# A four-layer block on one core: where the next batch's inputs, the shared expert and the output are put

## The chip, the core and the metric

The kernel runs on one core of one Trainium2 chip. The core has a matrix engine (TensorE, in the profile PE), a vector engine (VectorE, DVE), an engine for activation functions (ScalarE, ACT), a general one (GpSimd, POOL) and a queue engine (SyncE, SP), each with its own instruction queue worked off in order; sixteen DMA engines move data. PE reads from the on-chip memory SBUF and writes to PSUM, which has eight banks of 128 partitions by 512 float32. The metric is the device time of one execution in microseconds, the median of three runs.

## The reference

Four residual steps over x of shape (4, 512, 512) in float32: an attention, a gated feed-forward net with ternary weights, a state-space scan, and a second attention followed by a mixture of experts.

```python
def reference(...):
    x = L0_attn_x                                   # (4, 512, 512) float32
    x = x + _L0_attn_ref(_layernorm(x), W_qkv, W_o)           # 16 heads of 32, rotary, causal
    x = x + _L0_ffn_ref(_layernorm(x), w1, w3, w2)            # ternary weights, hidden 1365
    x = x + _L1_attn_ref(_layernorm(x), W_xproj, W_dt, b_dt, A_log, D_param)
    x = x + _L1_ffn_ref(_layernorm(x), ...)

# _L0_ffn_ref
g = silu(x @ w1q.T) * (x @ w3q.T);  return g @ w2q.T

# _L1_attn_ref: a scan over the tokens, 16 states per channel
delta = softplus((xz[..., :128] @ W_dt.T) + b_dt)
h = exp(delta * A) * h + delta * B_t * x_t;  y_t = sum(h * C_t);  return y + x * D_param

# _L1_ffn_ref: attention with a latent, then a mixture of experts
h = x + attention(rmsnorm(x, ln1_w), ...)
out = h + moe(rmsnorm(h, ln2_w), ...)
# moe: a shared expert for every token, and the 2 best of 7 experts, weighted
expert_ffn(x, wg, wu, wd) = (silu(x @ wg) * (x @ wu) / 8) @ wd        # inner size 256
return shared + combined
```

## The kernel before

B = 4 batches of T = 512 tokens with C = 512 channels; P = 128, and NT = NK = 4 tiles of tokens or channels. The residual x of batch b lies in SBUF as `xs[b]` all the time. The kernel is written in a framework that places the waits itself. Where a block stands under `manual_schedule(engines={PE})`, PE's instructions keep the order of the program; the other engines get an order from the framework's planner, which starts what is ready by its own estimate, earlier program text first. That order is then fixed. Every helper whose work is spread over a stage is a Python generator: each `next` emits the instructions up to its next `yield`, at that place of PE's order. PSUM is cut into two pairs of banks (`pair`, also `half_pair`, the first bank of a pair) and four single ones (`bank`); a new tile of a kind waits until one of its places is free.

**First attention** (0 to 430 us): not touched.

**Feed-forward** (430 to 751 us, lines 594 to 715). For each batch b and each of NF = 11 slices f of the hidden size, `gated` multiplies into the two banks of a pair `pg` (gate, then up; L651, 16 records, high and low parts), ACT applies Silu (L656), DVE multiplies (L657), and the product is cut into a high and a low part (L662, L663); `down` of the slice before adds into four banks `ys` (L669). `part(n)` is called three times a slice: n = 3f between gate and up, 3f + 1 after up, 3f + 2 after down. It advances `between`, which is `prepare(b - 1, ...)` (lines 495 to 588): the preparation of the scan for the batch before. `prepare` normalises (`make`), transposes (L131), projects (`pd`, `pb`, `pz`: L520, L529, L551), and computes softplus with Exp (L555), three DVE operations per channel tile on a tile `u` (L559 to L561), Ln (L563), and `finish` (L568 to L571: delta, its store, the product `ux`); `turn_out` transposes ux (L576), copies it to the one buffer `st` and stores it (L579). Those of Exp, Ln and Silu that follow one another on ACT load another table each time (1.28 us). `coming` is `inputs(b + 1)`, the norm and the transposes (`tpf`, L633) of the next batch's inputs; it is advanced once at the end of each slice from f = 4 on, right after part(3f + 2). In batch 3 there is no next batch, and `part` leaves out n = 2 only.

**Scan** (751 to about 1120 us, lines 812 to 971): 128 steps (batch, state, half). `prepare` of batch 3 goes on inside it: two of its pieces and then five stand ahead of the first step, one more after every second step.

**Second attention** (to about 1624 us). `soften`, `turn` and `weigh` run over 128 pairs of heads. `leave(b, oT)` follows for the batch before: four output projections (L1031), h = h + y (L1034), a store of h to the DRAM tensor `acc` (L1036), the square sum (L1038), the norm with ln2 (L1045), transposes, the store to `hrows` and the router. At the very end stand two pieces of `leave(3)`, then `shared(0)`, then the rest of `leave(3)`.

**Shared expert** `shared(b)` (lines 979 to 1009): transposes h by token tiles into hT, for each of two halves i of the inner size gate and up in the two banks of one pair (L990, eight records each), Silu (L995), product (L997); then four down projections (L1004) and the addition to xs[b] (L1008). `shared(1)` and `shared(2)` run beside the routing work.

**Routed experts** (about 1682 to 1905 us): 38 tiles of 128 places. For each, GpSimd gathers rows of `hrows` (L1386), PE runs the expert, and GpSimd adds the weighted rows to `acc` with an accumulating scatter (L1427); scatters follow one another. Here PE isn't ordered by hand. **The end:** `shared(3)`, and for each of 16 token tiles a load of `acc` on SP (L1449), an addition to xs (L1450), and a store to `out` on ACT's queue (L1451), all ordered by the planner.

## Time and profile before

| what | us |
|---|---|
| median of three runs (1941.34 to 1942.90) | 1942.84 |
| the profiled execution | 1946.77 |
| its span | 1945.0 |
| PE busy | 1764.7 |
| DVE busy | 1145.5 |
| ACT busy | 948.2 |
| GpSimd busy | 580.9 |
| PE waits in 425 to 745 us for DVE's sil | 8.0 |
| PE waits for ACT's hid / hTe in the shared experts | 4.4 / 4.5 |

In a line of the timeline stand the start, the duration, the engine, the line of the program, the operation, output and inputs, how many are merged, and in brackets how long the engine stood idle before it and who released it. Float32 matmuls over 512 columns appear as two records of some 0.43 us each; in the feed-forward stage one record is issued every 0.233 us. In a row of a stretch stand its length, busy time and number of instructions of PE, PE's weight loads, DVE, ACT and POOL, then the granted clock of PE as a share of full speed, the mean busy share of the DMA engines, and GB/s.

### The profile page before, as it was taken

The page shows a single profiled execution, that of the slowest core. Times are in us where ns is not written, and L with a number is a line of the kernel's source. Part 1 is how long each engine was busy: PE and PEld are TensorE (multiplying, and loading weights), DVE is VectorE, ACT ScalarE, POOL GpSimd, SP SyncE. Part 2 cuts the span into 40 slices and gives each one's busy share as a digit, 9 for nine tenths or more (in the row PEclk, how much of TensorE's full clock was granted, in tenths as well). Part 3 has the DMA queues.
Part 4 walks back from the last instruction along what each step waited for, and adds up shares of the span by engine and source line. Part 5 has one row for each costly group of instructions (what it writes and reads, how often), then busy time and mean ns, then how long its engine had stood idle before and what let it go on. Part 6 is the DMA issues. An engine that isn't in the chain of part 4 may idle for free. (4 is left out here: it accounts for less than half of the span.)

```text
span 1945.0 us, 26741 instructions
## 1 busy us (share of the span) xinstructions
PE 1764.7 (91%) x9970; PEld 1060.5 (55%) x9970; DVE 1145.5 (59%) x1849; ACT 948.2 (49%) x1945; POOL 580.9 (30%) x391
## 2 busy tenths in 40 slices
PE   7999999989999897967887889999999988999997
PEld 3433343337666665766776645555555544545443
DVE  6456435666454646999998865564655734322223
ACT  2434433332242436978999836665665732111110
POOL 2221212110202014867998910101000000244430
PEclk9999999999999998989999978999999999999998
DMA  7003200111010104123411100010001006255546
GB/s 245 8 1 99 69 1 1 44 30 47 1 39 7 44 1 152 54 100 89 143 56 46 43 1 1 1 44 1 33 23 38 29 11 235 74 93 91 91 72 190
DMA packets 70884, 114.24 MB, mean 59 GB/s; under 512 B 7962, under 2 KB 26778, under 8 KB 70756
## 3 DMA queue, kind: packets, MB, share of 16 engines
q1 hardware_dynamic: 59796, 88.02, 14.1%
q0 software_dynamic: 8656, 20.32, 5.9%
q10 hardware_dynamic: 2304, 4.20, 0.6%
q8 instruction: 80, 1.31, 0.3%
q14 instruction: 48, 0.39, 0.1%
HBM read 81.18 MB, written 31.33 MB: 58 GB/s over the span
## 5 line engine op out<-in xcount | busy, mean ns | idle before, releaser
L872 POOL TENSOR_TENSOR hc<-h,cb 128x1024 f32<-128x1024 f32 x128 | 303.2, 2410 | 43.3 <-DVE h L861 20.9
L861 DVE TENSOR_TENSOR_SCAN h<-da,bu 128x512 f32<-128x512 f32 x256 | 289.7, 1197 | 15.0 <-ACT da L845 6.9
L853 PE MATMUL bu<-ident,bu 128*128 128x128 f32 x1024 | 165.0, 290 | 55.5 <-DVE h L861 32.7
L271 PE MATMUL pq<-wqkv,hT 128*128 128x512 f32 x384 | 181.2, 620 | 0.7 <-ACT hT L132 0.7
L853 PEld LDWEIGHTS bu<-ident,bu 128*128 128x128 f32 x1024 | 121.7, 147 | 88.6 <-ACT bu L839 49.3
L845 ACT ACTIVATE da<-delta_l,am 128x511 f32<-128x511 f32 x256 | 165.9, 739 | 4.2 <-DVE h L861 4.2
L839 ACT ACTIVATE bu<-dxT,bts 128x512 f32<-128x512 f32 x256 | 165.7, 738 | 0.0
L1101 ACT ACTIVATE pr<-scd,nm 128x128 f32<-128x128 f32 (+3 forms) x256 | 133.1, 528 | 56.3 <-DVE nm L1098 53.6
L651 PE MATMUL pg<-hTh,w 128*128 128x512 f32 (+1 forms) x352 | 148.7, 422 | 9.3 <-DVE sil L657 8.0
L885 PE MATMUL ys<-ident,hc 128*128 128x128 f32 x1024 | 143.4, 285 | 13.4 <-POOL hc L872 11.2
L651 PE MATMUL pg<-hTl,w 128*128 128x512 f32 (+1 forms) x352 | 140.7, 400 | 0.2 <-DVE hTl L639 0.2
L1400 PE MATMUL pgr<-wgu,gTe 128*128 x304 | 137.1, 593 | 0.0
L885 PEld LDWEIGHTS ys<-ident,hc 128*128 128x128 f32 x1024 | 121.6, 147 | 21.7 <-POOL hc L872 18.0
L351 ACT ACTIVATE pt<-sc 128x1024 f32<-128x1024 f32 (+3 forms) x128 | 84.2, 698 | 84.2 <-PE sc L346 81.7
L271 PEld LDWEIGHTS pq<-wqkv,hT 128*128 128x128 f32 x384 | 72.1, 196 | 94.6 <-issue 86.3
L1090 PE MATMUL scd<-qkTd 32*128 32x512 f32 (+3 forms) x512 | 108.3, 504 | 12.9 <-ACT pr L1101 11.9
L102 POOL TENSOR_TENSOR ri_ln<-ri_ln,minus_half 128x4 f32<-128x4 f32 (+1 forms) x17 | 16.9, 994 | 302.6 <-DVE ri_ln L101 298.4
L1098 DVE TENSOR_REDUCE nm<-scd 128x2 f32<-128x256 f32 (+3 forms) x128 | 104.2, 815 | 0.0
L1113 PEld LDWEIGHTS tpd<-ident,pr 128*128 128x128 f32 x640 | 70.4, 145 | 61.0 <-issue 41.5
L1113 PE MATMUL tpd<-ident,pr 128*128 128x128 f32 x640 | 102.2, 292 | 0.6 <-ACT pr L1101 0.6
L352 POOL TENSOR_SCALAR_AFFINE_SELECT pt<-pt 128x512 f32<-128x512 f32 x64 | 43.5, 679 | 196.2 <-ACT pt L351 196.2
L1093 DVE TENSOR_TENSOR scd<-scd,neg 128x256 f32<-128x256 f32 x128 | 54.9, 430 | 69.8 <-PE scd L1090 67.7
(260 smaller groups left out, 3109.1 us busy)
## 6 DMA issues: line engine op xcount, KB each, us to landing
cb<-c_rows SPq DMA_DIRECT2D x64, 256.0 KB, 3.2
q_w<-in_w2T SPq DMA_DIRECT2D x20, 256.0 KB, 2.8
deltas<-delta SPq DMA_DIRECT2D x16, 256.0 KB, 2.1
dxs<-st SPq DMA_DIRECT2D x16, 256.0 KB, 2.5
delta_l<-deltas SPq DMA_DIRECT2D x4, 1024.0 KB, 9.0
dxT<-dxs SPq DMA_DIRECT2D x4, 1024.0 KB, 7.1
acc<-h SPq DMA_DIRECT2D x16, 256.0 KB, 2.0
hrows<-h SPq DMA_DIRECT2D x4, 1024.0 KB, 4.3
```

Source lines behind the costliest of these rows:

```text
L271: nc.tensor.matmul(y, inputs_T[b][:, k, t * P : (t + 1) * P], wqkv[:, k, s * C : (s + 1) * C], start=k == 0, stop=k == NK - 1,)
L651: nc.tensor.matmul(pg[:rows, i, :], w[:, k, f * P : f * P + rows], part[:, k, :], start=k + m == 0, stop=k + m == NK,)
L839: nc.scalar.activation(row, dxT[:, t, :], AF.Copy, scale=bts[:, b, t * NS + n : t * NS + n + 1])
L845: nc.scalar.activation(da[:, k, 1:], delta[:, k, 1:], AF.Exp, scale=am[:, k, n : n + 1])
L853: nc.tensor.transpose(bu[i][:, t * P : (t + 1) * P], scaled[b, n][t][:, k * P : (k + 1) * P], ident)
L861: nc.vector.tensor_tensor_scan(h[:, i, :], decays[b, n][:, 2 * half + i, :], bu, 0.0, ALU.mult, ALU.add)
L872: nc.gpsimd.tensor_tensor(hc, states.pop((b, n, half)), weighed[b, n].unsqueeze(1).to_broadcast([P, 2, T]), ALU.mult)
L885: nc.tensor.matmul(sums[b][t][:, k * P : (k + 1) * P], hc[:, i, t * P : (t + 1) * P], ident, is_transpose=True, start=n == 0 and k == 0, s ...
L1090: nc.tensor.matmul(sc[:, i, :w], qkT[at, g, t * P : w], qkT[at, NG + g, :w], start=True, stop=True)
L1101: nc.scalar.activation(pr[:, i, :w], sc[:, i, :w], AF.Exp, bias=nm[:, i : i + 1], accum_out=sums[b, g][:, t, 2 * p + i : 2 * p + i + 1],)
L1113: nc.tensor.transpose(tp[:, j * P : (j + 1) * P], pr[:, i, j * P : (j + 1) * P], ident)
L1400: nc.tensor.matmul(pg, gT[:, k, :], wgu[:, bass.ds(e, 1), k, :].rearrange("p e o -> p (e o)"), start=k == 0, stop=k == NK - 1,)
```

## The change

`prepare` is cut into 23 pieces in place of 30: the rows of tiles 2 and 3 are made after the second transpose, two channel tiles of u go together, Ln stands in one piece with the first two `finish`, and every later `finish` with a `turn_out`. In the feed-forward stage `part` gives the places n = 14, 17, ..., 32 to `coming` alone while there is a next batch, and leaves out n = 2, 3, 5 in every batch.

`shared` transposes by channel slices: one slice of all four token tiles fills a bank and is copied as a whole. Gate and up get a pair each. What is done with the result is a parameter: for batches 0 to 2 it is added to xs and xs is stored to `acc`. `leave` adds h to xs at once; only batch 3 is stored to `acc` there. At the end of the second attention the four transposing pieces of `shared(0)` come first, then four pieces of `leave(3)`, then the rest of both in turn.

At the end `acc` holds the whole sum for batches 0 to 2, and SP copies it to `out` from DRAM to DRAM, 1 MB each. The four tiles of batch 3 are loaded back into the place of hs[2]; `shared(3)` now stands under an order by hand for PE, DVE and ACT, adds its result to them, and ACT's queue stores four tiles.

```diff
--- before.py
+++ after.py
@@ -508,12 +508,14 @@
             nc.gpsimd.tensor_tensor(ud, row, dpar, ALU.mult)
             nc.gpsimd.tensor_tensor(x[:, t, :], x[:, t, :], ud, ALU.add)
 
+        make(0)
+        make(1)
+        yield
         for t in range(NT):
-            if t % 2 == 0:
-                make(t)
-                make(t + 1)
-                yield
             transpose_into(uT, rows.pop(t), t * P, spot=spot)
+            if t == 1:
+                make(2)
+                make(3)
             yield
         pd = spot("pd")
         for k in range(NK):
@@ -559,9 +561,9 @@
             nc.vector.tensor_scalar(u, e[:, k, :], 1.0, -1.0, ALU.add, ALU.add)
             nc.vector.tensor_tensor(u, e[:, k, :], u, ALU.subtract)
             nc.vector.tensor_tensor(delta[:, k, :], delta[:, k, :], u, ALU.add)
-            yield
+            if k % 2 == 1:
+                yield
         nc.scalar.activation(e, e, AF.Ln, bias=1.0)
-        yield
         scaled = {}
 
         def finish(k):
@@ -578,14 +580,14 @@
             nc.scalar.copy(st.rearrange("p t q -> p (t q)"), tp)
             nc.sync.dma_start(by_tokens(dxs, b)[:, :, k * P : (k + 1) * P], st)
 
+        finish(0)
+        finish(1)
+        yield
         for k in range(NK):
-            finish(k)
+            turn_out(k)
+            if k + 2 < NK:
+                finish(k + 2)
             yield
-            if k > 0:
-                turn_out(k - 1)
-                yield
-        turn_out(NK - 1)
-        yield
 
     def half_pair(name):
         return pair(name)[:, 0, :]
@@ -684,8 +686,11 @@
 
 
 
+
                 def part(n):
-                    if n not in ((2, 3, 5) if b < B - 1 else (2,)):
+                    if n % 3 == 2 and n > 3 * 4 and b + 1 < B:
+                        next(coming, None)
+                    elif n not in (2, 3, 5):
                         next(between, None)
 
 
@@ -705,8 +710,6 @@
                             ys = [bank(f"y{t}") for t in range(NT)]
                         down(b, *pending.pop(0), ys)
                     part(3 * f + 2)
-                    if f >= 4:
-                        next(coming, None)
                 for job in pending:
                     down(b, *job, ys)
                 for t in range(NT):
@@ -976,26 +979,38 @@
             sh[name] = dw.tile(shape, F32, tag=tag, name=name)
             nc.sync.dma_start(sh[name], by_rows(a[name]))
 
-    def shared(b, pool, tag):
+    def keep(b, t):
+
+        n = b * NT + t
+        nc.sync.dma_start(acc[n * P : (n + 1) * P, :], xs[b][:, t, :])
+
+    def add_shared(b, t, y):
+        nc.vector.tensor_tensor(xs[b][:, t, :], xs[b][:, t, :], y, ALU.add)
+        keep(b, t)
+
+    def shared(b, pool, tag, put=add_shared):
 
         hT = far.tile([P, NK, T], F32, tag="hT", name="hTe")
-        for t in range(NT):
-            transpose_into(hT, hs[b][:, t, :], t * P)
+        for k in range(NK):
+
+            tp = bank("tp")
+            for t in range(NT):
+                nc.tensor.transpose(tp[:, t * P : (t + 1) * P], hs[b][:, t, k * P : (k + 1) * P], ident)
+            nc.scalar.copy(hT[:, k, :], tp)
             yield
         hid = pool.tile([P, NI, T], F32, tag=tag, name="hid")
         for i in range(NI):
-            pg = pair("pge")
             for s, w in enumerate((sh["sh_gate"], sh["sh_up"])):
+                pg = pair("pge")[:, 0, :]
                 for k in range(NK):
                     nc.tensor.matmul(
-                        pg[:, s, :], w[:, k, i * P : (i + 1) * P], hT[:, k, :],
-                        start=k == 0, stop=k == NK - 1,
+                        pg, w[:, k, i * P : (i + 1) * P], hT[:, k, :], start=k == 0, stop=k == NK - 1
                     )
                 if s == 0:
-                    nc.scalar.activation(hid[:, i, :], pg[:, 0, :], AF.Silu)
+                    nc.scalar.activation(hid[:, i, :], pg, AF.Silu)
                 else:
                     nc.vector.scalar_tensor_tensor(
-                        hid[:, i, :], pg[:, 1, :], 0.125, hid[:, i, :], ALU.mult, ALU.mult
+                        hid[:, i, :], pg, 0.125, hid[:, i, :], ALU.mult, ALU.mult
                     )
                 yield
         for t in range(NT):
@@ -1005,7 +1020,7 @@
                     y, hid[:, i, t * P : (t + 1) * P], sh["sh_down"][:, i, :],
                     start=i == 0, stop=i == NI - 1,
                 )
-            nc.vector.tensor_tensor(xs[b][:, t, :], xs[b][:, t, :], y, ALU.add)
+            put(b, t, y)
             yield
 
     scans.close()
@@ -1022,7 +1037,6 @@
 
         def leave(b, oT):
 
-
             h = hs[b]
             ss = d2.tile([P, NT], F32, tag="ss", name="ss")
             for t in range(NT):
@@ -1032,8 +1046,9 @@
                         y, oT[:, k, t * P : (t + 1) * P], wow[:, k, :], start=k == 0, stop=k == NK - 1
                     )
                 nc.vector.tensor_tensor(h[:, t, :], h[:, t, :], y, ALU.add)
-                n = b * NT + t
-                nc.sync.dma_start(acc[n * P : (n + 1) * P, :], h[:, t, :])
+                nc.vector.tensor_tensor(xs[b][:, t, :], xs[b][:, t, :], h[:, t, :], ALU.add)
+                if b == B - 1:
+                    keep(b, t)
                 sq = d2.tile([P, C], F32, tag="row", name="sq")
                 nc.scalar.activation(sq, h[:, t, :], AF.Square, accum_out=ss[:, t : t + 1])
                 if t == NT - 1:
@@ -1187,9 +1202,12 @@
                 if at >= 7:
                     next(come, None)
 
-            for _ in range(2):
+            filler = shared(0, d1, "lat")
+            for _ in range(NK):
+                next(filler)
+            for _ in range(NT):
                 next(left)
-            for _ in shared(0, d1, "lat"):
+            for _ in filler:
                 pass
             for _ in left:
                 pass
@@ -1441,14 +1459,22 @@
                 turn_hidden(i)
 
 
-        for _ in shared(3, e1, "hid"):
-            pass
-        for b in range(B):
-            for t in range(NT):
-                n = b * NT + t
-                nc.sync.dma_start(hs[b][:, t, :], acc[n * P : (n + 1) * P, :])
-                nc.vector.tensor_tensor(xs[b][:, t, :], xs[b][:, t, :], hs[b][:, t, :], ALU.add)
-                nc.scalar.dma_start(out[n * P : (n + 1) * P, :], xs[b][:, t, :])
+        back = hs[B - 2]
+        for t in range(NT):
+            n = (B - 1) * NT + t
+            nc.sync.dma_start(back[:, t, :], acc[n * P : (n + 1) * P, :])
+        for b in range(B - 1):
+            nc.sync.dma_start(out[b * T : (b + 1) * T, :], acc[b * T : (b + 1) * T, :])
+
+        def add_and_store(b, t, y):
+            n = b * NT + t
+            nc.vector.tensor_tensor(back[:, t, :], back[:, t, :], y, ALU.add)
+            nc.scalar.dma_start(out[n * P : (n + 1) * P, :], back[:, t, :])
+
+        engines = {mybir.EngineType.PE, mybir.EngineType.DVE, mybir.EngineType.Activation}
+        with tc.manual_schedule(engines=engines):
+            for _ in shared(B - 1, e1, "hid", add_and_store):
+                pass
     latter.close()
```

## The prediction

> **What bounds the kernel now.** I read the page first, then waits and timeline of four stages.
>
> ```profile
> span 1945.0 us, 26741 instructions
> PE 1764.7 (91%) x9970; PEld 1060.5 (55%) x9970; DVE 1145.5 (59%) x1849; ACT 948.2 (49%) x1945; POOL 580.9 (30%) x391
> PEclk9999999999999998989999978999999999999998
> ```
>
> TensorE (PE) carries the kernel outside the scan (some 762 to 1120 us, where ScalarE, VectorE and GpSimd are full). PE runs in an order written by hand, so what counts is where it stands still, and what that does to its clock. First the feed-forward stage (430 to 751 us; timeline of PE, one row of granted clock, timelines of ScalarE and VectorE in batch 3):
>
> ```profile
> 554.13 0.80 PE L651 MATMUL pg<-hTh,w 128*128 128x512 f32 x1 [2.84 <-DVE sil L657]
> 568.98 0.50 PE L651 MATMUL pg<-hTh,w 128*128 128x512 f32 x1 [1.10 <-DVE sil L657]
> 639.06 0.60 PE L651 MATMUL pg<-hTh,w 128*128 128x512 f32 x1 [2.83 <-DVE sil L657]
> ...
> 639.00:643.00 4.00, 3.94 (x10) 3.12 (x11) 3.90 (x8) 0.62 (x1) 0.00 (x0) 0.57 0.00 0
> ...
> 718.17 1.92 ACT L555 ACTIVATE e<-e 128x2048 f32<-128x2048 f32 x1
> 728.17 1.28 ACT L563 ACT_TABLE_LOAD   x1 [0.75 <-DVE u L560]
> 729.47 1.92 ACT L563 ACTIVATE e<-e 128x2048 f32<-128x2048 f32 x1
> 733.46 0.63 PE L576 MATMUL tpd<-ident,ux 128*128 128x128 f32 x4 [1.25 <-DVE ux L571]
> ```
>
> In batches 1 and 2 PE waits twice for a PSUM pair that the gate still holds, because Exp and Ln of the inserted scan preparation sit before Silu on ScalarE; after the longer gap the clock is 0.57 for 4 us. In batch 3 the last four lines are one chain: Exp, four groups of VectorE work, table load, Ln, ux, and the first turned-out slice, for which PE already waits.
>
> Then the end of the second attention (timeline), and the end of the kernel (timeline, then DMA share and GB/s of two stretches):
>
> ```profile
> 1584.69 3.70 PE L990 MATMUL pge<-hTe,sh_gate 128*128 128x512 f32 x8 [1.45 <-ACT hTe L132]
> 1589.08 3.70 PE L990 MATMUL pge<-hTe,sh_up 128*128 128x512 f32 x8 [0.69 <-ACT hid L995]
> 1618.29 1.99 PE L131 MATMUL tp<-ident,h 128*128 128x128 f32 x9 [3.69 <-DVE h L1045]
> ```
>
> ```profile
> 1915.16 16.99 SPq L1449 DMA_DIRECT2D h<-acc  x16
> 1918.62 9.63 ACTq L1451 DMA_DIRECT2D out<-x  x8
> 1928.30 0.60 ACT L995 ACTIVATE hid<-pge 128x512 f32<-128x512 f32 x1 [15.95 <-DVE x L1450]
> 1941.10 0.69 DVE L1450 TENSOR_TENSOR x<-x,h 128x512 f32<-128x512 f32 x1
> ...
> 1925.00:1930.00 5.00, 3.99 (x6) 1.21 (x5) 2.69 (x4) 0.60 (x1) 0.00 (x0) 0.50 1.06 405
> 1930.00:1935.00 5.00, 5.00 (x10) 2.08 (x8) 1.03 (x3) 0.00 (x0) 0.00 (x0) 0.70 1.05 405
> ```
>
> The last shared expert's Silu stands 16 us behind output DMAs on ScalarE's queue; PE idles and falls to half clock. Meanwhile 8 MB go in and out at 405 GB/s.
>
> The profiled run took 1946.77 us, its span and 1.77 around it; the median of the runs is 1942.84, so 3.93 lower. I work out a difference on the trace and apply it to the median.
>
> **Feed-forward, batches 1 and 2.** The preparation has 23 pieces for 30. With three positions per slice (n = 3f to 3f+2) and 2, 3, 5 left out, before its piece k ran at n = k+2; now seven positions belong to coming alone, and the pieces fill the other 23: last projection n = 19 (18), Exp 21 (19), u 22 and 24 (20 to 23), Ln with two finishes 25 (24 to 26), first turn-out 27 (27). Slice 6's Silu is now asked for before Exp, so the 2.84 wait should go, and with it the slow clock: at 0.57 over 4 us, 4 x 0.43 = 1.7, of which I count 1.5. The 1.10 goes as well. Gain 5.4 a batch. The price is at the turn-out: from the last projection to n = 27 PE has 8 positions of 1.87 (24 matmul records of 0.233 per slice, a third of it) and three coming transposes of 0.6, 16.8 us. The chain needs Abs 0.7, table 1.28, Exp 1.92, four u groups of 1.85, table 1.28, Ln 1.92, add and product 1.4: 15.9, plus some 3 of gate and coming work between: 2.1 us of stall. One more us for slices that now turn out in adjacent positions: st has one buffer, and its DMA takes 2.5 us (dxs row of the page). So 5.4 - 3.4 = 2.0 a batch, **-4 us**; bounds -9 (no stall) and +3 (5.5 us of stall, which also slows the clock).
>
> *A rule against the row:* the Trainium skill, "TensorE: Matmul & The Clock Gate", Part 1, says the clock falls after an idle window of about 3.4 us. By it a 2.84 us gap costs only itself and this part comes to -1. The trace shows 0.57 after a 2.83 us gap, so I keep -4.
>
> **Feed-forward, batch 3.** No coming here, so the pieces are not spread: before, piece k ran at n = k, now at n = k+2, and the turn-out moves from n = 25 to n = 22, while Exp moves from 17 to 18. Its first row (n = 4 for 3) loses a wait of 1.55 and some 0.3 more. PE then reaches n = 22 at the old time 726.5 - 1.8 = 724.7. The chain ends no earlier than now: Exp's end at 719.6 to 720.1, u groups 7.4, sil and gl of one slice 1.4, table and Ln 3.2, add and product 1.4: 733.0 to 733.5, as in the trace (733.3). PE waits 8.3 us. From there it has slices 6 to 10 of down (5 x 1.83 with the pending ones counted) and 8 to 10 of gate and up (3 x 3.74), three turn-outs of 0.6 and the short ends: the trace takes 17.8 from the turn-out to 751.3, and one slice more (5.6) stands behind it now. 733.1 + 23.4 + 2 for the slow clock after the gap (half speed for 4 us at 757 to 761) + 1 for st = 759.5, so **+8 us**; bounds +4 and +12. What queues behind the waiting transposes on PE is the whole rest of the stage, and after it the norm of x3 and the first scan.
>
> **Scan.** Preparation of batch 3 ends at step 31 (45), same work. Half of pd now precedes the first transposes: ACT copy 0.6 and two records, some 1.9 us; hidden by GpSimd, whose first hc starts only at 768.67 while the scan was at 762.62; without that cover +1.9. **0**, bounds -3 and +3.
>
> **Second attention.** Twelve additions x<-x,h of 0.69 enter VectorE in batches 0 to 2 (8.3 us), the acc stores leave SP. VectorE is some 60% busy there, but PE waits for softmax (scd on pr, 11.9 in total). Bounds 0 and 8.3; near the lower, **+1.5**. At its end the filler comes first: four slices transposed, all four y, then gate, up, down, during which VectorE norms h. From 1574.20 to the router at 1621.70 are 47.5 us. What PE must do: 1.9 + 16 x 0.854 + 24 x 0.854 + 1.9 = 38.0; with 1.2 for the down wait and the last copy 39.2: **-8.3**; this holds the waits 1.45, two of 0.69, and 3.69. Four more additions and four stores stand where nothing waits.
>
> **Shared experts 1 and 2.** Slices let gate start when PE is through transposing, and up has its own pair: 1.48 + 2 x 0.69 = 2.86 for expert 1, 0.69 for expert 2 (its others are covered by routing work): **-3.6**. Their eight acc stores stand on SP's queue behind additions that end by 1683.8, after the last weight load (issued at 1649.4), and land, 2.0 us each, before the first scatter at 1695.5. The routed tiles (1684 to 1905, PE 224 of 225 us) don't change.
>
> **The end.** The last scatter lands at 1915.02 in either kernel. PE: transposes from 1905.26, gate from 1907.2, 16 x 0.854 to 1920.9, Silu and product 1.0, eight of 0.854 to 1928.0, addition 0.7; then, as now from the last addition (1941.8) to the end, 3.2: not before 1932. DMA: SP's queue holds the loads and copies behind the last scatter, and nothing behind them; four loads landed by 1919.6 (2.7 latency and 1 MB), then 3.15 MB DRAM to DRAM, of which the trace has no row, and 1.05 MB of stores. By the nearest row, 405 GB/s: 7.8 us, hidden, end 1932. *The rule against it:* the Trainium skill, "DMA: Bandwidth & Descriptors", Latency and other measured facts, gives 207 to 214 GB/s for copies between HBM tensors: 14.7 us, stores 2.6, completion 1.5, end 1938.4. The 405 are loads and stores side by side, each touching HBM once; I take 1936, between: **-9**, bounds -13 and -6.
>
> **Sum:** -4 + 8 + 0 + 1.5 - 8.3 - 3.6 - 9 = -15.4; 1942.84 - 15.4 = 1927.4.
>
> **Rivals.**
> *The batch 3 stall doesn't come* (VectorE's planned order brings ux sooner) and copies are fast: -15.4 - 8 - 4 = -27.4, 1915. Against: Exp, u and Ln alone fill 12 us.
> *The same stall in all batches*: turn-outs wait 8 us and slow the clock in batches 1 and 2, 2 x 7 more: -1.4, 1941. For it: the chain needs 18.9 by my own count; against: three more positions than in batch 3.
> *Slower: the DRAM copies become the end.* Without the tail the rest is worth -6.4. To end 3.9 later than before, the copies would have to run until 1955 on the old axis: 33 us for 3.15 MB, 95 GB/s. If one copy were given to few of the 16 engines (one is 405/16 = 25 GB/s), it costs 124 us, some 2040. Against: every load and store of the trace runs over 128 partitions and reaches full rate; for it: a copy with no partition side is not in the trace.
>
> **How the numbers follow.** The case above 0.55, its own range 1919 to 1936; no stall 0.17; stall everywhere 0.18; DRAM copies 0.10. 0.2% (3.9 us) is about what a measurement tells from no change. Faster: 0.54 + 0.17 + 0.06; same: 0.01 + 0.09; slower: 0.03 + 0.10. Range 1915 to 1943: leaves out the slow copies and the edges of both stall cases.
>
> **What would show it.** Right: no wait of 2.8 for sil near 554 and 639; a wait of 6 to 9 us for ux in batch 3; no wait of pge for hid or hTe; hTr transposes without 3.69; last Silu before the first store; acc to out at 200 to 400 GB/s. Wrong: out<-acc still landing after the last out<-h, or waits for ux in all batches, or scd waits well above 11.9.

## The result, and the profile after

The changed kernel takes 1934.61 us, the median of 6 runs (1929.99 to 1941.33), beside 1942.87 us for the kernel before in the same session: a ratio of 0.9958, 95% interval 0.9943 to 0.9973. It is 8.3 us faster, where 15.4 were forecast (1927.4, range 1915 to 1943).

The profiled executions took 1941.33 us (after) and 1946.77 us (before). The first is the slowest of its 6 runs and the second as slow as the slowest of the kernel before in that session (1946.82), so the two traces differ by 5.4 us and not by 8.3. The top of the page of after:

```profile
span 1939.6 us, 26716 instructions
PE 1764.7 (91%) x9970; PEld 1063.5 (55%) x9970; DVE 1143.7 (59%) x1849; ACT 946.0 (49%) x1945; POOL 580.8 (30%) x391
PEclk9999999999999998978999987999999999999999
```

PE's busy time is the same to the tenth of a microsecond as before. Everything that moved is waiting and clock, so it has to be found stage by stage. Each stage below is cut at the same instruction in all kernels (the end of the last x<-y,sc_w,x of a batch, the first pl, the first PE instruction of the end of attention, logit, the first pgr, the end of the last yr). Two columns are experiments that come below: before with the feed-forward part of the change alone, and after with that part taken back.

| stage, us | before | after | forecast | part alone | part taken back |
|---|---|---|---|---|---|
| feed-forward batch 1 | 86.2 | 89.3 | -2 | 89.1 | 83.6 |
| batch 2 | 85.0 | 89.4 | -2 | 84.6 | 85.1 |
| batch 3 | 81.1 | 90.2 | +8 | 90.4 | 81.1 |
| scan | 369.1 | 372.8 | 0 | 368.9 | 369.4 |
| second attention | 452.4 | 452.2 | +1.5 | 451.2 | 452.2 |
| its end, to logit | 50.1 | 41.3 | -8.3 | 50.1 | 41.1 |
| routing, shared experts 1 and 2 | 60.0 | 55.6 | -3.6 | 60.0 | 55.6 |
| routed experts | 221.2 | 221.2 | 0 | 221.2 | 221.2 |
| the end | 39.6 | 26.6 | -9 | 36.1 | 27.1 |

The lower half of the table did what was forecast, and somewhat more. The upper half, feed-forward and scan, lost 20 us in these two traces in place of 4. First the feed-forward stage: PE's waits from the end of batch 0 to the end of batch 3 (what PE waited for, us in all, times, longest), then six lines of the timelines of VectorE, PE and ScalarE (fp32r is the view's name for the type of the high and low parts).

```profile
PE tpd L578 <- DVE ux L573: 9.1, 1, 9.1
PE tpd L578 <- DVE hTl L641: 6.2, 2, 3.1
PE y L671 <- DVE gl L665: 4.0, 6, 1.2
PE pg L653 <- DVE sil L659: 2.8, 2, 1.4
PE y L671 <- ACT gh L664: 2.5, 2, 2.0
PE pg L653 <- ACT st L580: 0.5, 1, 0.5
```

```profile
568.68 0.68 DVE L573 TENSOR_TENSOR ux<-delta,uT 128x512 f32<-128x512 f32 x1
569.89 0.68 DVE L641 TENSOR_TENSOR hTl<-tpf,hTh 128x512 fp32r<-128x512 f32 x1
570.72 0.63 PE L578 MATMUL tpd<-ident,ux 128*128 128x128 f32 x4 [3.15 <-DVE hTl L641]
585.26 0.59 ACT L580 COPY st<-tpd 128x512 f32<-128x512 f32 x1 [2.44 <-DMA dxs<-st]
661.33 1.12 PE L578 MATMUL tpd<-ident,ux 128*128 128x128 f32 x4 [3.06 <-DVE hTl L641]
742.97 1.09 PE L578 MATMUL tpd<-ident,ux 128*128 128x128 f32 x4 [9.13 <-DVE ux L573]
```

The waits of the first list are 25.1 us; the same view of before adds up to 13.4 (sil 7.9 in four waits, row_s 1.5, gl 1.4, ux 1.3, three others 1.3). The forecast wait for ux in batch 3 is there (9.1, 8.3 forecast). The waits for sil, 2.84 and 1.10 a batch, were to go; one of 1.4 a batch is left. The first turned-out slice of batch 1 waits 3.15 us, from 567.57 to 570.72. Its ux is ready at 569.36, 1.8 us after PE stood ready; what ends the wait is hTl, the coming inputs' work, at 570.57. Batch 2 is the same (1.8 us for ux, ended by hTl at 3.06). And gh waits on ScalarE behind the copy into the single st buffer, which waits 2.44 us for its store.

Then the clock (us of the stretch, busy us of PE and of the other engines, granted clock, DMA share, GB/s):

```profile
571.50:575.00 3.50, 3.50 (x13) 2.76 (x11) 1.47 (x3) 0.95 (x2) 0.00 (x0) 0.51 0.59 210
588.50:592.00 3.50, 3.50 (x10) 2.69 (x9) 3.50 (x8) 0.00 (x0) 0.00 (x0) 0.52 0.00 0
660.00:667.50 7.50, 6.17 (x19) 5.13 (x20) 4.37 (x8) 2.13 (x3) 0.00 (x0) 0.54 0.45 162
738.50:746.00 7.50, 3.03 (x10) 2.63 (x11) 4.30 (x7) 2.97 (x3) 0.00 (x0) 0.54 0.33 118
```

Each of the four long new waits is followed by a stretch at half clock, or is still going on when it begins (the one of 9.13). Taking the share below full clock as half speed, the stretches last 2 x 0.49 x 3.5 = 3.4 us, 3.4, 6.9 and 6.9. Where PE is busy all through it, 3.4 us at half clock cost 1.7. Before, there were two such stretches of 3.4 us in these batches, now six units of it.

The scan, where VectorE's recurrence h sets the pace, has the same single buffer in it, because the preparation of batch 3 goes on there (ScalarE, then VectorE):

```profile
888.67 0.58 ACT L580 COPY st<-tpd 128x512 f32<-128x512 f32 x1 [5.00 <-DMA dxs<-st]
892.41 2.33 DVE L864 TENSOR_TENSOR_SCAN h<-da,bu 128x512 f32<-128x512 f32 x2 [5.75 <-ACT da L848]
```

The copy waits 5.00 us for the store of the slice before, and everything behind it on ScalarE with it, so that VectorE stands for 5.75 us. Before, the slices were further apart, and the copy waited 0.76 us.

The lower half, end of the second attention and end of the kernel (timelines; then one stretch with DMA share and GB/s):

```profile
1597.01 13.90 PE L1045 MATMUL y<-wow,oTd 128*128 128x512 f32 x32
1610.74 3.60 PE L1006 MATMUL pge<-hTe,sh_gate 128*128 128x512 f32 x8
1614.18 3.60 PE L1006 MATMUL pge<-hTe,sh_up 128*128 128x512 f32 x8
1631.61 1.91 PE L131 MATMUL tp<-ident,h 128*128 128x128 f32 x16
```

```profile
1921.60 1.74 SPq L1465 DMA_DIRECT2D h<-acc  x4
1923.39 1.86 SPq L1467 DMA_DIRECT2D out<-acc  x3
1925.07 0.60 ACT L1010 ACTIVATE hid<-pge 128x512 f32<-128x512 f32 x1 [6.27 <-PE pge L1006]
1931.21 5.49 ACTq L1472 DMA_DIRECT2D out<-h  x4
1935.64 0.69 DVE L1471 TENSOR_TENSOR h<-h,ye 128x512 f32<-128x512 f32 x1 [1.03 <-PE ye L1019]
```

```profile
1925.00:1935.00 10.00, 10.00 (x24) 4.16 (x23) 2.75 (x4) 0.60 (x1) 0.00 (x0) 1.00 1.00 360
```

The brackets of 1.45, 0.69 and 3.69 are gone from the end of attention: y, gate, up and the router's transposes follow one another without a gap. At the end the last Silu (1925.07) runs before the first store is issued (1931.21), the last addition ends at 1936.3, and the kernel 3.3 later. The DMA engines are full (share 1.00) from 1925 to 1935, and the last packet of the copies ends at 1935.65, before the last addition.

### The profile page after: what moved, and what is told of

The parts are those of the page before. It is cut to its first block, busy times and chain, and to the rows that moved or that the text cites. A ratio compares the mean times of both kernels' runs of the same rounds, so it can differ in the third digit from the quotient of the medians.

```text
span 1939.6 us, 26716 instructions
## 1 busy us (share of the span) xinstructions
PE 1764.7 (91%) x9970; PEld 1063.5 (55%) x9970; DVE 1143.7 (59%) x1849; ACT 946.0 (49%) x1945; POOL 580.8 (30%) x391
## 3 DMA queue, kind: packets, MB, share of 16 engines
q10 hardware_dynamic: 576, 1.05, 0.1%
## 5 line engine op out<-in xcount | busy, mean ns | idle before, releaser
L864 DVE TENSOR_TENSOR_SCAN h<-da,bu 128x512 f32<-128x512 f32 x256 | 289.5, 1197 | 19.4 <-ACT da L848 12.2
L856 PEld LDWEIGHTS bu<-ident,bu 128*128 128x128 f32 x1024 | 122.7, 148 | 79.9 <-ACT bu L842 42.9
L888 PE MATMUL ys<-ident,hc 128*128 128x128 f32 x1024 | 144.4, 286 | 16.0 <-POOL hc L875 14.0
L351 ACT ACTIVATE pt<-sc 128x1024 f32<-128x1024 f32 (+3 forms) x128 | 84.1, 697 | 84.2 <-PE sc L346 81.7
L271 PEld LDWEIGHTS pq<-wqkv,hT 128*128 128x128 f32 x384 | 72.0, 196 | 94.7 <-issue 86.2
L1105 PE MATMUL scd<-qkTd 32*128 32x512 f32 (+3 forms) x512 | 108.3, 504 | 12.9 <-ACT pr L1116 11.9
```

The costliest lines, as they stand in the source:

```text
L271: nc.tensor.matmul(y, inputs_T[b][:, k, t * P : (t + 1) * P], wqkv[:, k, s * C : (s + 1) * C], start=k == 0, stop=k == NK - 1,)
L856: nc.tensor.transpose(bu[i][:, t * P : (t + 1) * P], scaled[b, n][t][:, k * P : (k + 1) * P], ident)
L864: nc.vector.tensor_tensor_scan(h[:, i, :], decays[b, n][:, 2 * half + i, :], bu, 0.0, ALU.mult, ALU.add)
L888: nc.tensor.matmul(sums[b][t][:, k * P : (k + 1) * P], hc[:, i, t * P : (t + 1) * P], ident, is_transpose=True, start=n == 0 and k == 0, s ...
L1105: nc.tensor.matmul(sc[:, i, :w], qkT[at, g, t * P : w], qkT[at, NG + g, :w], start=True, stop=True)
```

## The experiments

### The feed-forward part taken back, and alone

Taken back: `prepare` in 30 pieces and the old places, all else as changed. Alone: the kernel before with these lines of the change.

```diff
             def part(n):
-                if n % 3 == 2 and n > 3 * 4 and b + 1 < B:
-                    next(coming, None)
-                elif n not in (2, 3, 5):
+                if n not in ((2, 3, 5) if b < B - 1 else (2,)):
                     next(between, None)
...
                 part(3 * f + 2)
+                if f >= 4:
+                    next(coming, None)
```

> The changed kernel with the feed-forward part of the change taken back: the preparation in 30 pieces, the places of between and coming as before, everything else (slices, two pairs, sums by token, the end) as changed. Theory A (the 23 pieces and their places cost what the two traces show up to the scan's end, some 0.8 + 3.1 + 4.3 + 9.1 + 3.6 = 21 us, and the rest of the change is untouched by it): the four feed-forward batches take 86, 85 and 81 us again for batches 1 to 3, and the time is 1934.6 - 21 = 1914, from 1911 to 1919. Theory B (what was lost ahead of the scan's end is partly taken up later, since the later stages start from queues that are less far on): stages up to the scan's end come back as before, but those after it grow, and the time is 1922 or more.

> The kernel before with the feed-forward part of the change alone. Theory A: 1942.9 + 17 to 21 = 1960 to 1964, with the waits of PE for ux (9 us in batch 3), for hTl and for gh in the same places as in the changed kernel. Theory B: less than 1955. My own forecast for these steps was +4 (1947); if that comes out, the two profiled executions misled and the loss lies elsewhere.

Taken back: 1922.33 us (1916.83 to 1925.14), ratio to before 0.9886, interval 0.9864 to 0.9908. Alone: 1956.60 us (1954.90 to 1960.23), ratio 1.0070, interval 1.0053 to 1.0087. So by the medians the feed-forward part costs 1934.6 - 1922.3 = 12.3 us one way and 1956.6 - 1943.5 = 13.1 us the other; the forecast for it was +4. All that is not the feed-forward part gains 1943.5 - 1922.3 = 21.2; the forecast for that was 19.4.

The first result meets theory B's number (1922 or more); the second lies between the two (B: less than 1955, A: 1960 to 1964), its 13.1 below the 17 to 21 of theory A. But theory B's mechanism, that later stages take the loss up, is not what the traces show: in the table the later stages of the two experiments are those of the kernel that each was made from, but for the last one of the part alone (36.1 for 39.6). What was too large was the 21 us that I had read off the two traces. Part of it was the clock of one execution, and here it is plain to see. Batch 2 took 89.4 us in after and 84.6 with the part alone, with the same instructions in the same order and the same wait for hTl. PE in that run:

```profile
659.83 0.66 PE L578 MATMUL tpd<-ident,ux 128*128 128x128 f32 x4 [3.06 <-DVE hTl L641]
```

The wait of 3.06 is the same to the hundredth, but in this run the clock stays at 1.00, and in after 6.9 us of half clock follow. All slow stretches of one trace begin on one grid of 3.413 us: those of after begin at 571.58, 588.65, 660.33 and 738.84, which lie 5, 21 and 23 such units apart. So cut the stretch around the wait on that grid (first two rows: after; last two: the part alone):

```profile
656.92:660.33 3.41, 1.35 (x6) 0.75 (x4) 2.15 (x4) 2.21 (x3) 0.00 (x0) 1.00 0.18 68
660.33:663.74 3.41, 2.41 (x8) 2.12 (x9) 3.35 (x6) 0.59 (x1) 0.00 (x0) 0.50 0.23 86
```

```profile
655.13:658.55 3.42, 1.64 (x8) 0.98 (x6) 1.88 (x4) 2.50 (x3) 0.00 (x0) 1.00 0.09 35
658.55:661.96 3.41, 2.13 (x12) 1.83 (x13) 3.41 (x7) 0.59 (x1) 0.00 (x0) 1.00 0.31 119
```

In after, 2.1 of the 3.06 us fall into one unit, in which PE is busy for 1.35 us, a share of 0.40; with the part alone they are divided into 0.48 and 0.63. The Trainium skill, "TensorE: Matmul & The Clock Gate", Part 1, says that the clock is set from activity windows of some 3.4 us that run freely. The traces agree. Over the 14 traces here, from 420 to 745 us, half clock followed each of the 38 units in which PE was busy for a share of 0.40 or less, and none of the 1174 with 0.80 or more; of the 137 between, 9. What decides between 0.40 and 0.80 stays open. So the page's "idle window" needn't be idle: a gap of 2 us in the wrong place is enough, and one of 3 us may cost nothing. Batch 2's 4.8 us are then 2.9 of half clock behind this wait, 0.8 of a slow stretch that reaches over from batch 1, and a wait of 1.05 for gl at its start (the first two are estimates, half of PE's busy time in the slow stretches).

The scan is another matter. It took 372.8 us in after, and 371.8, 368.9, 372.5, 372.8, 368.8 and 372.8 in the six other traces that have the 23 pieces and the single st; there the copy into st waits 5.0, 3.3, 2.8, 4.8, 4.7, 2.8 and 4.6 us for the store of the slice before. In the three traces with 30 pieces (369.1, 369.4, 367.7) the wait is 1.0 or less. From the 33rd to the 129th of h's 256 instructions, where the slices are turned out, after took 149.7 us, the kernel before 145.3, and the changed kernel with two buffers for st (below) 144.4. So what after lost in the scan is a cost of the change while st has one buffer; how large it is differs from trace to trace.

### Coming's places kept in batch 3

```diff
-                if n % 3 == 2 and n > 3 * 4 and b + 1 < B:
+                if n % 3 == 2 and n > 3 * 4:
                     next(coming, None)
```

> The changed kernel, with coming's own places in all four batches: batch 3 loses its places at n = 14, 17, 20 ... for the preparation too, so that the first turning out comes at n = 27 and no longer next to the last exponential. Theory A (the wait for ux is a matter of how many positions lie between Exp and the first turning out): the wait of 9.1 us in batch 3 falls to 1 to 4, batch 3 takes 84 to 86 us in place of 90.2, and the time falls by 4 to 7 to about 1929. Theory B (DVE and ACT are too full in batch 3 for ux to come sooner, wherever the piece is placed): the wait moves with the piece and the time stays within 2 us of 1934.6. Theory C: batch 3 becomes like batches 1 and 2 (89.3) and only 1 us is won.

1928.40 us (1927.17 to 1931.11), ratio to before 0.9924 (0.9907 to 0.9940): 6.2 us less than the changed kernel. Batch 3 took 81.2 us, no longer than before the change, and its waits (same view as above, batch 3 alone) are

```profile
PE tpd L578 <- DVE ux L573: 3.1, 1, 3.1
PE pg L653 <- ACT st L580: 0.3, 1, 0.3
PE y L671 <- DVE gl L665: 0.2, 1, 0.2
```

Theory A: the wait for ux is a matter of how many places lie between Exp and the first turning out. Five more places (n = 27 for 22), of some 1.9 us each, took 6.0 off the wait, and the clock kept 1.00 through the batch (the wait fell into two units of the grid, with PE busy for 0.45 and 0.64 of them). The batch is shorter than the 84 to 86 us of the expectation.

### Two buffers for st

```diff
-            st = pool.tile([P, NT, P], F32, tag="st", name="st")
+            st = pool.tile([P, NT, P], F32, tag="drT" if k % 2 else "st", name="st")
```

The second buffer is the one of drT, which is no longer needed then.

> The changed kernel, with two buffers in turn for st, so that ACT's copy of the turned dx no longer waits for the store of the one before. Theory A (ACT's in-order queue behind that copy is what makes PE wait for gh, 2.0 us in batch 1): the wait for gh at the end of batch 1 is gone and the batches 0 to 2 win 1 to 2.5 us each: 3 to 6 in all. Theory B (ACT and DVE are late for other reasons, the Ln and the casts): the wait for gh goes over to another operand and the time stays within 1.5 us.

1927.77 us (1926.09 to 1929.00), ratio 0.9917 (0.9900 to 0.9933), 6.8 us less than the changed kernel. Batch 1 took 84.8 us (89.3), batch 2 85.7 (89.4). PE's waits in batch 1:

```profile
PE tpd L578 <- DVE hTl L641: 3.1, 1, 3.1
PE pg L653 <- DVE sil L659: 1.4, 1, 1.4
PE tpf L635 <- ACT st L580: 0.3, 1, 0.3
PE y L671 <- DVE gl L665: 0.2, 1, 0.2
```

The 2.0 for gh is gone (and 1.2 for gl, at the start of the batch); hTl and sil are untouched. The clock was at 1.00 through the whole batch in this run, where after had a slow stretch behind hTl and another behind gh. Theory A holds for gh, but it looked in the wrong place for the rest: the largest single gain of the trace, which the expectation didn't count, is the scan, 365.8 us for 372.8. There the copies into st no longer wait for a store. That the wait for hTl left the clock alone is luck of the grid (0.46 and 0.62). How the 6.8 divide between scan, gh and clock these runs don't say.

The same two buffers in the kernel with the feed-forward part taken back:

> The changed kernel with the feed-forward part taken back (as in the first of these runs, 1922.3) and two buffers in turn for st. Theory A (the wait of ACT for st holds up the casts here too, 9.0 us of ACT's time in 5 waits): 1 to 3 us less, 1919 to 1921. Theory B (there the turning out is spread over ten pieces, and the waits of ACT are covered): within 1 us of 1922.3; PE's waits for sil, 8.0 us, come from the exponential alone.

1918.34 us (1914.88 to 1922.14), ratio 0.9877 (0.9856 to 0.9898). The median is 4.0 us lower, but the runs overlap with those without the second buffer (1916.83 to 1925.14), and the batches took 84.7, 85.0 and 81.1 us, not less. ScalarE no longer waits 8.0 us for the store, but PE's waits are the same: 7.9 us for sil, in four. So for the batches theory B, though the time lies below the numbers of both theories: where turning out is spread over ten places, the wait was covered, and the exponential is what holds PE. Whether the 4.0 is more than chance these runs can't say.

### Another order for the preparation

21 pieces in places of their own, on top of the changed kernel and two st. The pieces, in this order: norm, rows 0 and 1, T0 (transposes of row 0), T1 with rows 2 and 3, T2, T3, pd, pz 0 and 1, pz 2 and 3, Exp, pb, u 0 and 1, pbt, u 2, u 3, Ln, finish 0 and 1, four turn-outs. Their places:

```diff
             def part(n):
-                if n % 3 == 2 and n > 3 * 4 and b + 1 < B:
+                if n in (15, 20, 21, 23, 26, 29):
                     next(coming, None)
-                elif n not in (2, 3, 5):
+                elif n in (0, 1, 4, 5, 7, 8, 10, 11, 12, 13, 14, 16, 17, 18, 19, 22, 24, 25, 28, 31, 32):
                     next(between, None)
```

Exp (n = 13) and Ln (n = 22) come right after a Silu was handed to ScalarE, so that they have a slice of PE work before the next one is due; the first turning out is at n = 25 in every batch.

> The changed kernel with another order of the preparation inside the feed-forward: 21 pieces, both halves of pd, pb and of each pair of pz in one piece, the exponential at n = 13 and Ln at n = 22 (each right after a Silu has been given to ACT), B and C between them, the first turning out at n = 25 in all batches, coming at n = 15, 20, 21, 23, 26, 29, and two buffers in turn for st. Theory A (the loss is the order, not the number of pieces): no wait of PE for ux above 1 us, none for hTl in batches 1 to 3, batches 1 to 3 take 83 to 85, 83 to 85 and 80 to 82 us, and the time is 1915 to 1923. Theory B (DVE and ACT have too little room between two Silus for any order): the waits for sil, ux and hTl add up to as much as in the changed kernel (22 us), and the time is 1930 or more.

1914.60 us (1912.71 to 1915.13), ratio 0.9852 (0.9836 to 0.9868). The batches took 83.5, 83.2 and 81.7 us. PE's waits in batches 1 to 3, and the clock of each batch:

```profile
PE pz L630 <- DVE delta L632: 9.4, 6, 1.6
PE pg L754 <- DVE sil L760: 2.2, 2, 1.1
PE y L772 <- DVE gl L766: 1.1, 1, 1.1
```

```profile
498.59:582.04 83.45, 79.10 (x342) 57.54 (x341) 45.29 (x73) 33.60 (x47) 12.96 (x9) 1.00 0.08 26
582.04:665.20 83.16, 78.89 (x342) 57.53 (x341) 45.47 (x71) 33.59 (x47) 12.77 (x9) 1.00 0.08 26
665.20:746.88 81.68, 75.97 (x319) 54.47 (x317) 40.92 (x66) 31.24 (x43) 13.04 (x9) 1.00 0.09 29
```

Theory A: 25.1 us of waiting became 12.7, none for ux or hTl, no single one above 1.6 us, and no slow stretch in any of the three batches. Against the kernel with the two buffers alone (1927.77) it is 13.2 us less, and in its trace the three batches took 248.3 us for 260.1. DVE, ScalarE and PE do the same work in both, so this part was the order. The six waits of 1.6 are mine: I had put two products pz into one pair of banks, and the second is held until the first has been read.

The next kernel issues both products first:

```diff
             if k % 2 == 0:
                 pzs = pair("pz")
+                for s in (0, 1):
+                    nc.tensor.matmul(pzs[:, s, :], wdt[:, (k + s) * P : (k + s + 1) * P], drT, start=True, stop=True)
             pz = pzs[:, k % 2, :]
-            nc.tensor.matmul(pz, wdt[:, k * P : (k + 1) * P], drT, start=True, stop=True)
```

> The run with the preparation's own order (1914.6), with both products of a pair of pz issued before the first of them is read. There PE waits 6 times 1.56 us for delta: the second product of a pair is held until the first half of that pair has been read. Theory A (these waits are PE's own time, with nothing that takes them up): 9.4 us less, so batches 1 to 3 about 80.3, 80 and 78.5 us, and 1905 to 1908 us in all. Theory B (with the products sooner the exponential meets another wait, for sil or for ux, and the clock falls after it): 1910 to 1915.

1911.42 us (1909.53 to 1912.28), ratio 0.9825 (0.9812 to 0.9839): the fastest of all, 23 us below the changed kernel. The batches took 82.2, 82.2 and 80.5. Only a third of the 9.4 came, because the wait moved on, to sil and to the next pair (theory B):

```profile
PE pz L630 <- DVE delta L635: 3.6, 3, 1.2
PE pg L757 <- DVE sil L763: 3.4, 3, 1.1
```

### The end of the second attention, and the shared experts

The old order of the end, the rest as changed:

```diff
-            filler = shared(0, d1, "lat")
-            for _ in range(NK):
-                next(filler)
-            for _ in range(NT):
+            for _ in range(2):
                 next(left)
-            for _ in filler:
+            for _ in shared(0, d1, "lat"):
                 pass
```

> The changed kernel with the old order at the end of the second attention: two steps of leave, then shared expert 0, then the rest. If the order gives the 8.8 us of this stage: from PE's first instruction of it to logit 41.3 goes to 48 to 50 us, with waits of PE of 2 to 4 us for the slices of the last batch. If the slices (transposes by k, which need every token block) or the pairs gave it: 41 to 44 us. The later stages stay as they are.

The stage took 46.2 us (41.3): the order is worth 5.0 of the 8.8, and the slices and pairs the other 3.8. That is less than the 48 to 50 expected from the order alone, so neither of the two extremes holds. The wait of before is back, with a half clock behind it (3.38 us for transposes that take 1.91 in after):

```profile
1631.00 3.38 PE L131 MATMUL tp<-ident,h 128*128 128x128 f32 x16 [3.68 <-DVE h L1060]
```

This run also told something of the end, below. Its time was 1944.02 us in a single run.

Gate and up in one pair again, slices kept:

```diff
         for i in range(NI):
+            both = pair("pge")
             for s, w in enumerate((sh["sh_gate"], sh["sh_up"])):
-                pg = pair("pge")[:, 0, :]
+                pg = both[:, s, :]
```

> The changed kernel with gate and up of the shared expert again in one pair of banks, slices kept. If the two pairs saved what I counted (PE's wait for hid, 0.69 twice in each expert): each expert 1.4 us more: shared experts 1 and 2 together with the routing 55.6 to 58.4 us, the end 28.3 to 29.7, the stage with shared expert 0 41.3 to 42.7; 5 to 6 us in all. If the slices alone took the waits: within 0.5 us in each stage.

The three stages with a shared expert took 42.9 us (41.3), 58.5 (55.6) and 28.3 (26.6), 6.2 us more in all: the pairs do what was counted, and the waits are these (routing with experts 1 and 2, then the end):

```profile
PE pge L1007 <- ACT hid L1011: 2.1, 3, 0.7
PE pge L1007 <- ACT hid L1011: 1.4, 2, 0.7
```

The time was 1943.97 us in a single run, with upper stages as slow as in the profiled run of after.

### The end: order, or bytes and additions?

The kernel before with its whole last stage under an order written down by the code:

```diff
-        for _ in shared(3, e1, "hid"):
-            pass
-        for b in range(B):
-            for t in range(NT):
-                ...
+        with tc.manual_schedule(engines={PE, DVE, Activation}):
+            for _ in shared(3, e1, "hid"):
+                pass
+            for b in range(B):
+                for t in range(NT):
+                    ...
```

> The kernel before, with its last stage (shared expert 3 and the 16 loads, additions and stores) under an order of PE, DVE and ACT that is written down by the code, as the changed kernel has it, and nothing else of the change. Theory A (the 13 us of the end came from the bytes and additions that no longer follow the expert): the stage after the last yr goes from 39.6 to 37 to 40 us. Theory B (they came from the order in the queues): 27 to 32 us.

The stage took 40.6 us, 39.6 before and 36.1 with the feed-forward part alone, in single runs: theory A (a little above its 37 to 40). The Silu no longer stands behind output DMAs, the 5.5 us that PE waited for hid are gone, and PE is through at about 1925.4 (end of its last ye) with 15 us left to run:

```profile
1926.00 9.71 DVE L1452 TENSOR_TENSOR x<-x,h 128x512 f32<-128x512 f32 x16
...
1926.72 10.04 ACTq L1453 DMA_DIRECT2D out<-x  x16
```

The sixteen additions and stores now follow the expert, where before they had run beside it. The gain at the end comes from having only four of them left, and the sums of the other three batches made long before; the order in the queues, which the prediction showed as the reason, is worth nothing while the sixteen additions stand behind the expert. Whether the four additions would do as well in the planner's order, no run shows.

The copies acc to out by way of buffers on the chip:

```diff
-            nc.sync.dma_start(out[b * T : (b + 1) * T, :], acc[b * T : (b + 1) * T, :])
+            nc.sync.dma_start((hs[0], hs[1], xs[0])[b], by_tokens(acc, b))
+        for b in range(B - 1):
+            nc.sync.dma_start(by_tokens(out, b), (hs[0], hs[1], xs[0])[b])
```

> Not the store itself is left out but its way is changed: the three outputs of 1 MB go from acc to buffers on the chip and from there to out, in place of straight from acc to out. If the copies are hidden behind PE's last expert with room to spare: the stage after the last yr stays 26.6 to 27.2 us. If they are near the end: 8.4 MB in all (1 + 3 MB in, 3 + 1 MB out) at the 405 GB/s of the copies are 20.7 us from 1921.6, so that the stage grows by 2 to 5 us, and the last out ends after the last addition by more than 3.3 us.

> The changed kernel, with the three outputs of 1 MB taken from acc into buffers on the chip that nothing else reads any more, and from there to out, in place of straight from acc to out (the run before it took a buffer that the last expert still reads, so that its expert worked on other rows and waited for the load). If the copies are hidden behind PE's last expert with room to spare: the stage after the last yr stays 26.6 to 27.2 us. If they are near the end: 8.4 MB in all at the 405 GB/s of the copies are 20.7 us from the first issue, so that the stage grows by 2 to 5 us, and the last out ends after the last addition by more than 3.3 us.

The first of these loaded batch 2 into the buffer from which the last expert still had to read, so its expert worked on those rows and waited for them (1961.38 us, last stage 52.9); it says nothing of the question. The second took 1948.35 us in a single run, its last stage 35.6 us, 9.0 more than after. That is more than the 2 to 5 expected. PE was through as early as in after (the last addition begins 22.7 us after the last yr in both), and the last store could only be issued when its 1 MB had come in, 13.2 us after the issue; then everything runs at about 400 GB/s to the end (SP's timeline, a stretch):

```profile
1936.05 0.37 SPq L1469 DMA_DIRECT2D out<-x  x1
```

```profile
1936.00:1940.00 4.00, 0.00 (x0) 0.00 (x0) 0.00 (x0) 0.00 (x0) 0.00 (x0) 0.50 1.05 408
```

So the direct copies are hidden, but with little room. The run with the old order of leave shows it too: there the copies were issued at 1924.84, 4.3 us before PE's last ye starts (4.9 in after), and took 9.2 us to land (8.1). The stores of the last rows ran into them and took 4.5 us to land (3.3 in after), and the kernel ended 5.2 us after its last addition instead of 3.3. So in this run, with the copies 0.6 us later against PE, the stage took 1.9 us more (28.5).

## Why the prediction was half right

**Right.** *The end of the second attention* (-8.3, measured -8.8) and *shared experts 1 and 2* (-3.6, measured -4.3), with the waits named: undoing the order brought 5.0 us back, undoing the pairs 6.2 in three stages, in a single run each. *Feed-forward, batch 3* (+8, measured +9.1, wait 8.3 forecast and 9.1 measured): the chain from Exp to ux stood as worked out, and giving it back its places took 6.2 us off. *Second attention* (+1.5, measured -0.2): scd waited for pr 11.9 us, exactly as before, so the twelve additions were free.

**The step that failed: feed-forward, batches 1 and 2, and with it the scan.** By the medians, the whole feed-forward part cost 12.3 to 13.1 us where +4 stood; all else gained 21.2 where 19.4 stood. Less the 9.1 of batch 3, 3 to 4 us are left for batches 1 and 2 and the scan together, where -4 and 0 stood (how they divide, only single traces show). Of the gain of 5.4 a batch, a wait of 1.4 for sil stayed. Of the price, the stall for ux was sized about right (2.1 us, measured 1.8). What it left out is the neighbour: the coming input's cast came later than ux, and the wait was 3.1 us in each batch. ScalarE takes things in order and was in Ln, VectorE was in the finishes, and the pair of banks that coming's transposes had filled was not released for the turning out. The prediction had costed the chain of the moved pieces, and the neighbours only as "some 3 of gate and coming work". The st term (1 us a batch) was of the right kind, but its victim was wrong: behind the blocked copy stood gh, for which PE waited 2.0 us. And it was not carried over to the scan, where the turned-out slices moved together as well: "same work", 0, was forecast, and a copy that waited 5.00 us for its store held up VectorE (+3.6 in the trace, outside the bound of +3; in the seven traces where that copy waits 1.0 us or less, the scan took 365.8 to 369.4).

**The clock.** The prediction counted 1.5 us a batch as gained with the wait for sil. Waits of 2 to 3 us elsewhere brought the slow stretches back, and more of them in the profiled run. In the trace of after the upper half looks 7 us worse than the medians make it. The choice against the page's rule was right for the trace of before and too simple as a rule: there the wait of 2.84 lay within one unit of the grid (PE busy for 0.21 of it). In the kernel with the part taken back the same wait of 2.84, at 555.56, was divided between two (0.64 and 0.53), and the clock stayed at 1.00.

**The end** was mis-sized: -9 taken, -13.0 measured in the trace, the bound of the case in which the copies are hidden. The term was the copies: an end at 1936 on the old axis was taken, between the two rates. Their last packet ended at 1935.65 of the trace of after, 1928.1 on the old axis, near the 1927.4 of the faster rate (405 GB/s), and the last addition ended after it (1936.3). Part of the 13 is luck of the trace of before, as the same last stage took 36.1 us in the run with the feed-forward part alone. *The view shown for it*, the Silu 16 us behind stores, was a symptom: with the sixteen additions kept, removing it gained nothing. The sum held because it rested on what PE must still do; its terms add up to 1928.7 and not 1928.0, but the 1.0 for Silu and product was not paid, as the down projections followed the last up without a gap, so that PE was through at 1928.0.

**The rivals.** The rival "same stall in all batches" was nearest in kind: batches 1 and 2 do stall, for ux and then hTl, and for 3 us instead of 8. "No stall in batch 3" and "the copies become the end" fell; the latter by a margin of a microsecond or so.

## What to carry to other kernels

When pieces of work are put into the gaps of another loop, don't only cost their own chain: list for each in-order engine what stands directly behind the long instruction (here Ln and its table load), and which PSUM buffer that work holds, in every stage where the pieces run. Put long activations right after the activation that the main loop is waiting for, and give a copy that waits for a DMA a second buffer before anything else stands behind it. And read a difference of a few microseconds between two traces of a clock-gated engine only after setting the slow stretches of each beside each other.

## What the runs showed of the hardware that was not expected

The granted clock falls in units of 3.41 us that lie on one grid through a trace; 1.7 us are lost for each that PE works through. What counts is how busy PE was in one unit, and not the length of the gap: a share of 0.40 or less was followed by half clock in 38 of 38 cases, and the same 3.06 us wait cost nothing more in one execution and 6.9 us at half clock in another. The kernel whose three batches had no wait above 1.6 us had no slow stretch in them, and its four runs lie within 2.4 us, where six runs of the changed kernel spread over 11.

Three copies from DRAM to DRAM of 1 MB each, one instruction each, were through 12.3 us after the first issue, beside loads and stores. The DMA engines were full in that time and moved 360 GB/s (1925 to 1935 us). The same bytes by way of buffers on the chip ran at 400 to 408 GB/s but have to be moved twice, and the slowest load alone took 13.2 us. A figure for a shorter stretch can mislead: from 1924 to 1927 us the view gives 574 GB/s with a DMA share of 1.66, since it counts a packet where it starts.
